# A three-layer graph attention kernel on one core: another PSUM bank for one pick a round, the first copy of picked tiles on VectorE, and node work after the picks

## The chip, the core and the metric

The kernel runs on one NeuronCore of a Trainium2 chip. Its engines each follow their own queue of instructions in order and meet only at semaphores: PE (TensorE, the matmuls; PEld is its weight loader), DVE (VectorE), ACT (ScalarE), POOL (GpSimd, here the issuer of gathers) and SP (SyncE, the issuer of most other transfers). Matmuls write into PSUM, which has eight banks of 2 KB a partition; VectorE and ScalarE read it from there. The metric is device time in microseconds (us) of one execution.

## The reference

The inputs are a graph of N = 6250 nodes with 64 features each, and 206250 edges sorted by destination, with 64 features each. Three layers of graph attention follow, then a residual and a layer norm.

```python
def _transformer_conv(x, src, dst, edge_attr, Wq, bq, Wk, bk, Wv, bv, We, Ws, bs):
    q = x @ Wq + bq
    k = x @ Wk + bk
    v = x @ Wv + bv
    e = edge_attr @ We
    kj = k[src] + e
    alpha = jnp.sum(q[dst] * kj, axis=-1) / jnp.sqrt(jnp.float32(D))
    amax = jax.ops.segment_max(alpha, dst, num_segments=N)
    p = jnp.exp(alpha - amax[dst])
    denom = jax.ops.segment_sum(p, dst, num_segments=N)
    w = p / denom[dst]
    msg = (v[src] + e) * w[:, None]
    agg = jax.ops.segment_sum(msg, dst, num_segments=N)
    return agg + x @ Ws + bs
...
for i in range(L):
    x = _transformer_conv(x, src, dst, edge_attr, Wq[i], bq[i], Wk[i], bk[i], Wv[i], bv[i], We[i], Ws[i], bs[i])
    x = jax.nn.relu(x)
    if i < L - 1:
        x = _layer_norm(x, ln_gamma[i], ln_beta[i])
return jax.nn.log_softmax(x, axis=1)
```

## The kernel before

**Units.** The edges are cut into chunks of 768 (six tiles of 128), and four chunks make a unit: 67 whole units and a rest. For each layer, `main_path` walks over the units in a loop whose body has four quarters, j = 0 to 3, one chunk each. All engines follow the order in which this loop is written; nothing reorders it later. Several units are in flight: while unit u is turned, unit u-1 is scored and weighted, unit u-2 is summed, and source rows are collected for unit u+1.

**What one unit needs.** `turn` (L1679, L1682) transposes the source rows of a chunk on PE and copies them out with ScalarE. `scores` (L1692) multiplies them with the queries, one half of the columns into bank `s` and the other into `s` (layer 0) or `m` (layers 1 and 2). `most` (L1706, L1719) takes the maximum of each half on VectorE, and after the second half ScalarE takes the exponential (L1720). `weights` (L1734, L1737) transposes the probabilities into bank `p` and copies them out; `sums` (L1746, L1753) makes the weighted sums. `store` writes a unit's partial results.

**Picks.** Source rows come in two ways. Most tiles are gathered by index with a transfer that POOL issues (L601), once ScalarE has copied its indices into a gate (L633). The others are picked: all node rows of a window lie on chip (`parts`), VectorE writes one-hot columns (L1335, by `aim`), and PE multiplies (L1387, eight matmuls a pick, by `Picker.batch`). A pick gives 2 tiles of 128 rows with 4 candidates each, side by side in one PSUM bank. `evacuate` keeps the right one: a copy of candidate 0 (L1356, on ScalarE), then three predicated copies of candidates 1 to 3 over it (L1359, on VectorE). Then the bank is free. After a pair's last pick ScalarE swaps half of its rows in three copies (L1346 to L1348).

**Layer 0** makes four picks a unit, one each quarter, in banks p, p, s, p (the string `ppsp`). It also has the sorter to run: the edge features are put in the order of the picks by one-hot matmuls (L1074 on VectorE, L1085 and L1094 on PE), a few steps each quarter by `move`, half of them ahead of the pick and half after it; `evacuate` is called after the second half. Bank `s` is shared with the scores there, and bank `p` with the probabilities.

**Layers 1 and 2** make six or seven picks a unit (2, 1, 2, 1 or 2, 2, 2, 1 in the quarters) in bank `x`, which has two buffers; each is evacuated right after it is issued.

**Node work.** Whenever all edges of a group of four node blocks are done, `finish` works through the group in small steps (L1499 to L1577), and, but for the last layer, `project` (L1432 to L1448) makes the next layer's queries. `step` runs one step of the node work that layer 0 has active; `close_up`, in quarter 0, runs that and one step of every group that is being finished. In layers 1 and 2 `step` finds nothing to do, so that only `close_up` matters there.

Of the kernel before, what the change touches and what calls it, by code (L numbers as in the profile page):

```python
# [32 lines left out]
LB = 4  # L33
# [396 lines left out]
def main_path(  # L430
# [53 lines left out]
    nc = tc.nc  # L484
# [815 lines left out]
    class Picker:  # L1300
# [49 lines left out]
        def evacuate(self):  # L1350

            if not self.late:
                return
            k, pair, t, px, which = self.late.pop()
            found = loaded[self.layer, k][:, 2 * pair : 2 * pair + 2, t, 0]
            nc.scalar.copy(found, px[:, :, 0])  # L1356
            first = t * LB + 2 * pair
            for b in range(1, KB):
                nc.vector.copy_predicated(  # L1359
                    found,  # L1360
                    which[:, first : first + 2, b].bitcast(I32).unsqueeze(2).to_broadcast([P, 2, D]),
                    px[:, :, b],
                )
            if t == self.plan[k][pair] - 1:
                self.swaps.append((k, pair, t + 1))
# [6 lines left out]
        def batch(self, k):  # L1372

            for pair, most in enumerate(self.plan.get(k, ())):
                for t in range(most):
                    if not self.layer:
                        self.swap()
                    self.aim()
                    at, hot = self.hots[k, t]
                    bank = "x" if self.layer else "ppsp"[self.quarter]  # L1380
                    px = ps(bank).rearrange("p (s b d) -> p s b d", s=2, b=KB)
                    for v in range(2):
                        w = t * WT + v
                        those, b0 = parts[w // HALF], w % HALF * WB
                        for h in range(NH):
                            for i in range(2):
                                nc.tensor.matmul(  # L1387
                                    px[:, v].rearrange("p b d -> p (b d)"),
                                    hot[:, h, (2 * pair + v) * P : (2 * pair + v + 1) * P],
                                    those[:, i, b0 + h * KB : b0 + (h + 1) * KB, :].rearrange("p b d -> p (b d)"),  # L1390
                                    start=(h == 0 and i == 0),
                                    stop=(h == NH - 1 and i == 1),
                                )
                    self.late.append((k, pair, t, px, self.which[k]))
                    if not any(t < more for more in self.plan[k][pair + 1 :]):
                        self.free.append(self.hots.pop((k, t))[0])
                    if self.layer:
                        due = len(self.swaps)
                        self.evacuate()
                        self.swap(len(self.swaps) - due)  # L1400
                    self.aim()
                    yield
            self.which.pop(k, None)
# [491 lines left out]
    for layer in range(L):  # L1895
# [3 lines left out]
        def free(u, j):  # L1899
            lead = 2 * LB if not layer else min(2 * LB, LB + u)  # L1900
            release(layer, u * LB + j + (0 if not layer else 1) + lead, nc.scalar.copy)

        picker = Picker(layer)
        for u in range(NU - 2):
# [11 lines left out]
            for j in range(LB):  # L1916
                picker.quarter = j
                if j == 2:
                    line.weights(u - 1, 0)
                this.turn(j)  # L1920
                if j == 0:
                    line.refill(u - 2)
                free(u, j)
                if j == 0:
                    if layer:
                        line.most(u - 1, 0)
                        line.products(u - 1, 1, "m")
                    close_up()
                else:
                    if j == 1:  # L1930
                        line.store()
                    step()
                a, b = -(-n * j // LB), -(-n * (j + 1) // LB)
                move(pace - pace // 2)
                if not layer and (not j or j == 1 and placed(0, u + 1)):
                    line.most(u - 1, j)
                for _ in range(b - a):
                    next(picking, None)
                move(pace // 2)
                if not layer:  # L1940
                    picker.evacuate()
                if j == 0:
                    if layer:
                        line.most(u - 1, 1)
                    else:
                        line.products(u - 1, 1)
                        if not placed(0, u + 1):
                            line.most(u - 1, 1)
                    ask(layer, u + 1)
                    chunks[layer, u + 1].across()  # L1950
                if j == 2:
                    line.weights(u - 1, 1)
                    chunks[layer, u + 1].shade()
                    decode(layer, u + 2)
# [21 lines left out]
        u = NU - 2  # L1976
# [117 lines left out]
```

## Time and profile before

| | us |
|---|---|
| median of three runs | 4764.53 |
| the three runs | 4761.85 to 4769.58 |
| profiled execution, its own time | 4768.13 |
| span of its instructions | 4766.3 |
| TensorE clock granted, mean | 0.873 |

Busy time over the span is 3718.2 us (78%) on PE, 3073.9 (64%) on DVE, 2548.1 (53%) on ACT and 2659.0 (56%) on POOL. The steady stretch of layer 0 runs from 180 to 2290 us, that of layer 1 from 2363 to 3480 and that of layer 2 from 3600 to 4680.

A group of the profile stands for all instructions of one line, engine and shape: after the count come busy us and mean ns of one, then the idle time of that engine just before them and what ended it. In a timeline, "[2.71 <-DVE feat L1359]" says that the engine had idled 2.71 us and that the instruction of L1359 on VectorE ended the wait. In the view of waits a line gives engine, what waited, whom it waited for, the total in us, how often, and the longest. A wait for several semaphores is put down to the one that came last. The granted clock is a share of TensorE's full clock.

### The profile page before, as it was taken

How to read it: one execution, taken by the hardware profiler on the slowest of the kernel's cores; microseconds unless marked ns; L12 is line 12 of the kernel's file. 1: busy time of each engine (PE TensorE's matmuls, PEld its weight loads, DVE VectorE, ACT ScalarE, POOL GpSimd, SP SyncE). 2: the span in 40 equal slices, each digit the busy share in tenths (PEclk: the TensorE clock that was granted, in tenths of full speed). 3: DMA queues.
4: the chain of work that ended last, by engine and by line, in shares of the span. 5: the costliest groups of instructions: out<-in, count | busy, mean ns of one | idle time of the engine just before them, and what ended most of it. 6: DMA issues, size and time to landing. Idle time of an engine off the chain costs nothing.

```text
span 4766.3 us, 108288 instructions
## 1 busy us (share of the span) xinstructions
PE 3718.2 (78%) x34711; PEld 2645.0 (55%) x34711; DVE 3073.9 (64%) x10790; ACT 2548.1 (53%) x6962; POOL 2659.0 (56%) x2642
## 2 busy tenths in 40 slices
PE   4888777887878878788588777878867887777786
PEld 2444444444444445445467666666646666666664
DVE  5576666666667666666456666666655666666665
ACT  1344444444444444445466666666646666666665
POOL 5464454555544544455376666666637666666663
PEclk9888888888888888889688899999879888888887
DMA  5655455455555545555566666666655666666663
GB/s 124 175 156 146 127 150 144 131 151 141 144 149 142 144 136 146 141 137 161 131 163 174 162 166 166 176 170 168 171 153 147 175 163 162 166 163 173 162 164 96
DMA packets 783502, 728.92 MB, mean 153 GB/s; under 512 B 485192, under 2 KB 610050, under 8 KB 782928
## 3 DMA queue, kind: packets, MB, share of 16 engines
q1 hardware_dynamic: 630436, 508.46, 40.4%
q0 software_dynamic: 84224, 86.41, 9.4%
q10 hardware_dynamic: 68268, 127.03, 7.4%
q8 instruction: 283, 4.64, 0.4%
q14 instruction: 291, 2.38, 0.2%
HBM read 562.78 MB, written 158.68 MB: 151 GB/s over the span
## 4 chain that ended last, share of the span: by engine, by line


## 5 line engine op out<-in xcount | busy, mean ns | idle before, releaser
L601 POOL DMA_INDIRECT feat<-x,gate x1460 | 1447.5, 991 | 776.5 <-ACT gate L633 363.7
L601 POOL DMA_INDIRECT feat<-in_x,gate x1100 | 1138.3, 1035 | 1115.4 <-ACT gate L633 823.2
L1387 PE MATMUL ps_x<-parts,hot 128*128 128x256 f32 x6864 | 1096.5, 316 | 307.3 <-DVE feat L1359 184.7
L1359 DVE COPY_PREDICATED feat<-which,ps_x 128x128 f32<-128x128 int32 x2574 | 766.0, 302 | 792.2 <-ACT feat L1356 704.7
L1387 PEld LDWEIGHTS ps_x<-parts,hot 128*128 128x128 f32 x6864 | 987.6, 218 | 410.5 <-issue 156.1
L1682 ACT COPY featT<-ps_a 64x384 f32<-64x384 f32 x1588 | 751.7, 473 | 320.6 <-PE ps_a L1679 309.3
L1734 PE MATMUL ps_p<-ident,prob 128*128 128x128 f32 x1197 | 246.3, 323 | 330.3 <-DVE feat L1359 202.1
L1679 PE MATMUL ps_a<-ident,feat 128*128 128x128 f32 x2380 | 453.7, 303 | 32.2 <-DMA feat<-x,src_b 31.3
L1335 DVE TENSOR_SCALAR hot<-keys,rank 128x512 fp32r<-128x512 f16 (+1 forms) x1172 | 471.1, 469 | 1.6 <-DMA keys<-keyS 1.6
L1074 DVE TENSOR_SCALAR hit<-ruler,pos 128x384 bf16<-128x384 f16 x1608 | 447.9, 320 | 14.2 <-PE ps_m L1094 14.2
L1679 PEld LDWEIGHTS ps_a<-ident,feat 128*128 128x128 f32 x2380 | 308.3, 155 | 210.7 <-issue 181.8
L1720 ACT ACTIVATE prob<-prob,part 128x768 f32<-128x768 f32 x204 | 190.2, 932 | 385.3 <-DVE part L1719 371.2
L1734 PEld LDWEIGHTS ps_p<-ident,prob 128*128 128x128 f32 x1197 | 156.6, 162 | 385.9 <-issue 230.1
L1359 DVE COPY_PREDICATED feat<-which,ps_p 128x128 f32<-128x128 int32 x552 | 165.6, 300 | 303.5 <-ACT feat L1356 289.7
L1085 PE MATMUL ps_x<-hit,raw 128*64 128x384 bf16 x1608 | 321.4, 395 | 0.7 <-DVE hit L1074 0.5
L1356 ACT COPY feat<-ps_x 128x128 f32<-128x128 f32 x858 | 221.9, 266 | 175.2 <-PE ps_x L1387 156.5
L1746 PE MATMUL ps_g<-feat,probT 128*32 128x128 f32 x9672 | 312.8, 276 | 0.8 <-ACT probT L1737 0.8
L1085 PE MATMUL ps_x<-hit,rest 128*64 128x384 bf16 x1608 | 303.9, 374 | 0.0
L1085 PE MATMUL ps_x<-hit,end 128*64 128x384 bf16 x1608 | 301.4, 371 | 0.0
L1692 PE MATMUL ps_s<-featT,q 128*32 128x384 f32 x2134 | 249.7, 511 | 44.5 <-DVE most L1706 26.4
L1746 PEld LDWEIGHTS ps_g<-feat,probT 128*32 128x32 f32 x9672 | 262.6, 110 | 25.1 <-ACT probT L1737 2.5
L1737 ACT COPY probT<-ps_p 128x384 f32<-128x384 f32 x399 | 192.7, 483 | 129.7 <-PE ps_p L1734 126.5
(266 smaller groups left out, 5230.0 us busy)
## 6 DMA issues: line engine op xcount, KB each, us to landing
featT<-eaS SPq DMA_DIRECT2D x792, 192.0 KB
feat<-eaP SPq DMA_DIRECT2D x134, 768.0 KB
raw<-in_ea SPq DMA_DIRECT2D x536, 96.0 KB
eaS<-eT ACTq DMA_DIRECT2D x134, 384.0 KB
eaP<-feat ACTq DMA_DIRECT2D x128, 384.0 KB
shade<-maskS SPq DMA_DIRECT2D x198, 192.0 KB
keys<-keyS SPq DMA_DIRECT2D x66, 448.0 KB
keys<-keyS SPq DMA_DIRECT2D x66, 384.0 KB
```

The costliest lines, as they stand in the source:

```text
L601: nc.gpsimd.indirect_dma_start(out=feat[:, c, t, 0], out_offset=None, in_=xts[layer][:, :], in_offset=bass.IndirectOffsetOnAxis(ap=index[: ...
L1074: nc.vector.tensor_scalar(hit, ruler, self.pos[:, at : at + 1], None, ALU.is_equal)
L1085: nc.tensor.matmul(self.px[j * D : (j + 1) * D, :HE], self.parts[2 * h + i].thirds[part][:, j, t * D : (t + 1) * D], self.hits[h, 2 * i + ...
L1335: nc.vector.tensor_scalar(hot[:, h], keys[self.layer, k][:, first : first + n], rank[:, h : h + 1], None, ALU.is_equal)
L1356: nc.scalar.copy(found, px[:, :, 0])
L1359: nc.vector.copy_predicated(found, which[:, first : first + 2, b].bitcast(I32).unsqueeze(2).to_broadcast([P, 2, D]), px[:, :, b],)
L1387: nc.tensor.matmul(px[:, v].rearrange("p b d -> p (b d)"), hot[:, h, (2 * pair + v) * P : (2 * pair + v + 1) * P], those[:, i, b0 + h * KB ...
L1679: nc.tensor.transpose(pt[:, t * P : (t + 1) * P], rows[:, 2 * t * D : 2 * (t + 1) * D], ident)
L1682: nc.scalar.copy(featT[:, :, h, :], pt[h * D : (h + 1) * D, : n * P].rearrange("d (i e) -> d i e", e=P))
L1692: nc.tensor.matmul(p_s[rows, :w], self.q[:, rows], self.featT[j][:, cols], start=True, stop=True)
L1734: nc.tensor.transpose(p_t[:, t, :n], self.prob[:n, at : at + P], ident[:n, :n])
L1746: nc.tensor.matmul(p_g[rows, :].rearrange("n (h d) -> n h d", h=2), self.probT[:, t, rows], batch[:, j, t], start=(t == 0), stop=(t == sel ...
```

## The change

Three edits, all in `main_path`. First, `evacuate` makes the copy of candidate 0 on VectorE. Second, in layer 0 the second pick of a unit goes to bank `s` in place of `p`; the second half's `most` moves ahead of `step` and of the sorter's steps in quarter 1, since that pick needs the bank which `most` reads. Third, in layers 1 and 2 the picks of a quarter come straight after its turn, and `close_up` or `step` after the picks; in quarter 0 the second half's `most` now stands behind the first pick, and no longer behind all picks of the quarter.

```diff
@@ evacuate
-            nc.scalar.copy(found, px[:, :, 0])
+            nc.vector.tensor_copy(found, px[:, :, 0])
@@ batch
-                    bank = "x" if self.layer else "ppsp"[self.quarter]
+                    bank = "x" if self.layer else "pssp"[self.quarter]
@@ the loop over quarters
                 free(u, j)
+                if j == 0 and layer:
+                    line.most(u - 1, 0)
+                    line.products(u - 1, 1, "m")
+                if j == 1:
+                    line.store()
+                    if not layer and placed(0, u + 1):
+                        line.most(u - 1, 1)
+                a, b = -(-n * j // LB), -(-n * (j + 1) // LB)
+                if layer:
+                    for i in range(max(b - a, 1)):
+                        next(picking, None)
+                        if not i and not j:
+                            line.most(u - 1, 1)
                 if j == 0:
-                    if layer:
-                        line.most(u - 1, 0)
-                        line.products(u - 1, 1, "m")
                     close_up()
                 else:
-                    if j == 1:
-                        line.store()
                     step()
-                a, b = -(-n * j // LB), -(-n * (j + 1) // LB)
-                move(pace - pace // 2)
-                if not layer and (not j or j == 1 and placed(0, u + 1)):
-                    line.most(u - 1, j)
-                for _ in range(b - a):
-                    next(picking, None)
-                move(pace // 2)
                 if not layer:
+                    move(pace - pace // 2)
+                    if j == 0:
+                        line.most(u - 1, 0)
+                    for _ in range(b - a):
+                        next(picking, None)
+                    move(pace // 2)
                     picker.evacuate()
                 if j == 0:
-                    if layer:
-                        line.most(u - 1, 1)
-                    else:
+                    if not layer:
                         line.products(u - 1, 1)
                         if not placed(0, u + 1):
                             line.most(u - 1, 1)
```

On PE in layer 0 this is the second pick of one unit, between two steps of the sorter (`hot` are the one-hot columns, `parts` the node rows, `ps_p` and `ps_s` the banks):

```order
 L1094 LDWEIGHTS stamp_259
 L1094 MATMUL ps_m<-hit,stamp_259 32x384
-L1387 MATMUL ps_p<-parts,hot_18028 128x256 x8
+L1387 MATMUL ps_s<-parts,hot_18028 128x256 x8
 L1128 MATMUL ps_a<-ident,eT 128x128 x3
 L1085 LDWEIGHTS raw
```

The pick keeps its place in PE's order and changes its bank. On VectorE in layer 0, at the end of quarter 0 of a unit, the first pick leaves its bank and the second maximum follows:

```order
 L989 TENSOR_SCALAR spare<-spare 128x96
 L991 TENSOR_SCALAR spare<-spare 128x96
-L1359 COPY_PREDICATED feat<-which,ps_p 128x2x64 x3
+L1356 COPY feat<-ps_p 128x2x64
+L1359 COPY_PREDICATED feat<-which,ps_p 128x2x64 x3
+L1706 ISA prob,most<-ps_s,shade,most 128x384
+L1706 ISA most 128x1
+L1719 TENSOR_SCALAR part<-most 128x1
 L1074 TENSOR_SCALAR hit<-ruler,pos 128x384 x2
 L1042 TENSOR_TENSOR rest<-raw 128x384
```

The copy of L1356 has come to this engine, and the maximum of the second half (L1706, L1719) stands right behind the first pick; before, it stood eleven rows further on, behind the sorter's work of quarter 1. On VectorE in layer 1, quarter 0 of a unit with node work (L1519 and below are `finish`):

```order
 L1706 ISA prob,most<-ps_s,shade 128x384
 L1706 ISA most 128x1
+L1356 COPY feat<-ps_x 128x2x64
+L1359 COPY_PREDICATED feat<-which,ps_x 128x2x64 x3
+L1706 ISA prob,most<-ps_m,shade,most 128x384
+L1706 ISA most 128x1
+L1719 TENSOR_SCALAR part<-most 128x1
+L1356 COPY feat<-ps_x 128x2x64
+L1359 COPY_PREDICATED feat<-which,ps_x 128x2x64 x3
 L1519 TENSOR_TENSOR el<-mm,both 128x8
 L1522 TENSOR_TENSOR has<-el 128x4
```

Both picks of the quarter and the second maximum now stand ahead of the seven instructions of node work of this unit; before, they stood behind them, and the second maximum behind both picks.

## The prediction

> **What bounds the kernel now.** I read the busy time by stage first. The rows below are layer 0 and the steady parts of layers 1 and 2; the columns are the stretch, its length, and busy microseconds (with instruction counts) of PE, the weight loader, VectorE (DVE), ScalarE (ACT) and GpSimd (POOL), then the granted TensorE clock and DMA.
> ```profile
> core 0: us, PE busy (x) PEld busy (x) DVE busy (x) ACT busy (x) POOL busy (x), PEclk, DMA share, GB/s
> 180.00:2290.00 2110.00, 1703.95 (x15463) 1010.97 (x15466) 1412.28 (x5044) 1007.57 (x2675) 1075.94 (x1042) 0.86 0.53 145
> 2363.00:3480.00 1117.00, 899.04 (x8860) 745.76 (x8864) 715.79 (x2436) 686.77 (x1972) 731.79 (x739) 0.91 0.64 167
> 3600.00:4680.00 1080.00, 862.21 (x8545) 725.11 (x8546) 699.19 (x2400) 691.02 (x1942) 697.19 (x703) 0.89 0.64 166
> ```
> PE is busiest in every stage, at about 80%, so what matters is who ends PE's idle time: 406 us in layer 0, 218 us in each later layer. The view of waits, for PE alone, says it. Layer 0 (300 to 2280 us):
> ```profile
> PE ps_p L1734 <- DVE feat L1359: 200.3, 59, 5.1
> ```
> Layer 1 (2370 to 3480 us):
> ```profile
> PE ps_x L1387 <- DVE feat L1359: 100.9, 81, 2.8
> PE ps_p L1734 <- ACT prob L1720: 57.3, 53, 1.9
> PE ps_x L1387 <- ACT feat L1348: 31.7, 24, 2.5
> ```
> Layer 2 (3600 to 4690 us):
> ```profile
> PE ps_x L1387 <- DVE feat L1359: 83.7, 66, 3.5
> PE ps_x L1387 <- ACT feat L1348: 81.6, 39, 4.1
> PE ps_p L1734 <- ACT prob L1720: 52.8, 43, 1.9
> ```
> Columns are total, times, longest. Layer 0 has one wait that is half of all PE idle time: the transposes of the probabilities (L1734) want bank p, which a pick still holds. The later layers have 298 us at picks that wait for a bank of x (a pick's tile leaves it with L1359; the swaps of L1348 only end beside that), and 110 us for the exponential of L1720.
>
> **Layer 0, the bank.** One round around 1020 us, in order of time (start, length, engine, line):
> ```profile
> 1019.56 1.21 PE L1387 MATMUL ps_p<-parts,hot 128*128 128x256 f32 x8
> 1019.60 0.61 DVE L1706 CUSTOM_DVE_ANT_0 prob<-ps_s,shade,most 128x384 f32<-128x384 f32 x1
> ...
> 1020.44 0.94 ACT L1720 ACTIVATE prob<-prob,part 128x768 f32<-128x768 f32 x1 [1.18 <-DVE part L1719]
> ...
> 1023.26 0.28 ACT L1356 COPY feat<-ps_p 128x128 f32<-128x128 f32 x1
> ...
> 1023.58 0.97 DVE L1359 COPY_PREDICATED feat<-which,ps_p 128x128 f32<-128x128 int32 x3 [2.71 <-ACT feat L1356]
> ...
> 1024.69 0.52 PE L1734 MATMUL ps_p<-ident,prob 128*128 128x128 f32 x3 [2.71 <-DVE feat L1359]
> ...
> 1026.56 1.21 PE L1387 MATMUL ps_s<-parts,hot 128*128 128x256 f32 x8
> ```
> The second pick ends at 1020.8, yet its tile leaves bank p only at 1024.55: VectorE idles 2.71 us for a copy that stands in ScalarE's queue. PE then stands 2.71 us too, although the probabilities were ready at 1021.4. With that pick in bank s, L1734 needs of p only what the first quarter's pick left long before. Bank s takes the second pick once the second maximum (L1706) has read it, and that is now queued ahead of the quarter's other VectorE work. The third pick, also in s, must wait for the second's copies. It started at 1026.56, two sorting steps after L1734, so with PE 2.7 us earlier it would want s at 1023.9, 0.7 us before the copies ended; but those no longer queue on ScalarE, so they end some 2 us earlier. Of 200.3 us I take 170; bounds 0 (the wait moves to the third pick or to L1720) and 200.
>
> **Layer 0, the clock.** After such a stall PE is given a lower clock. Seven stalls in a row, the 3.4 us after each (clock: third number from the end):
> ```profile
> 1024.60:1028.00 3.40, 3.31 (x30) 2.49 (x32) 2.24 (x8) 2.31 (x7) 0.94 (x1) 1.00 1.11 215
> 1057.60:1061.00 3.40, 3.40 (x14) 1.68 (x14) 1.70 (x6) 2.22 (x7) 0.52 (x1) 0.50 1.06 236
> 1100.20:1103.60 3.40, 3.32 (x18) 2.04 (x18) 2.33 (x8) 2.14 (x7) 0.44 (x1) 0.50 0.50 166
> 1132.60:1136.00 3.40, 3.34 (x19) 2.12 (x19) 2.22 (x8) 2.17 (x7) 0.46 (x1) 0.56 1.12 247
> 1162.40:1165.80 3.40, 3.36 (x19) 1.90 (x20) 2.20 (x8) 2.41 (x7) 0.94 (x1) 0.58 1.03 246
> 1194.10:1197.50 3.40, 3.30 (x14) 1.70 (x14) 1.79 (x6) 2.13 (x7) 0.43 (x1) 0.50 0.89 270
> 1234.60:1238.00 3.40, 3.38 (x18) 2.03 (x18) 2.17 (x8) 2.21 (x7) 0.51 (x1) 0.50 0.55 170
> ```
> Mean 0.59, so 1.4 us of each stretch is lost; 59 times 1.4 is 83. The shorter idle gaps that stay may trip it too: I take 70, bounds 0 and 120. [...]
>
> **The first copy on VectorE.** These are groups by line: count, then busy and mean ns, then the idle time before them.
> ```profile
> L1359 DVE COPY_PREDICATED feat<-which,ps_x 128x128 f32<-128x128 int32 x2574 | 766.0, 302 | 792.2 <-ACT feat L1356 704.7 <-ACT gate L633 12.6 <-DMA feat<-x,gate 10.1
> L1359 DVE COPY_PREDICATED feat<-which,ps_p 128x128 f32<-128x128 int32 x552 | 165.6, 300 | 303.5 <-ACT feat L1356 289.7 <-ACT feat L1348 1.0
> L1359 DVE COPY_PREDICATED feat<-which,ps_s 128x128 f32<-128x128 int32 x180 | 54.4, 302 | 245.9 <-ACT feat L1356 241.7
> L1356 ACT COPY feat<-ps_x 128x128 f32<-128x128 f32 x858 | 221.9, 266 | 175.2 <-PE ps_x L1387 156.5 <-issue 3.0
> L1005 DVE COPY spare<-ps_a 128x96 f32<-128x96 f32 x16 | 3.9, 244 | 0.0
> L776 DVE COPY qs<-ps_a 64x128 f32<-64x128 f32 x3 | 0.8, 276 | 2.8 <-DMA qq<-qs 2.8
> ```
> VectorE takes 244 copies in layer 0 (552 + 180 over 3) and 858 later. Its nearest rows for a copy out of PSUM are 244 ns (96 columns) and 276 ns (128 columns, half the partitions): I take 276, so 304 us in all, 67 of them in layer 0, and ScalarE loses 266 ns each. In layer 0 that lies under the 531 us (289.7 + 241.7) in which VectorE stood waiting for ScalarE: nothing on the path; without that cover, 67. [...]
>
> **Layers 1 and 2.** One unit of layer 1 with no node work in it:
> ```profile
> 2706.07 3.17 DVE L1335 TENSOR_SCALAR hot<-keys,rank 128x512 fp32r<-128x512 f16 x8
> ...
> 2707.70 2.17 PE L1387 MATMUL ps_x<-parts,hot 128*128 128x256 f32 x16
> ...
> 2709.16 0.54 DVE L1706 CUSTOM_DVE_ANT_0 prob<-ps_s,shade 128x384 f32<-128x384 f32 x1
> ...
> 2709.64 2.02 DVE L1359 COPY_PREDICATED feat<-which,ps_x 128x128 f32<-128x128 int32 x6
> ...
> 2710.75 2.24 PE L1387 MATMUL ps_x<-parts,hot 128*128 128x256 f32 x16 [0.55 <-ACT feat L1356]
> ...
> 2712.40 0.94 ACT L1720 ACTIVATE prob<-prob,part 128x768 f32<-128x768 f32 x1 [1.75 <-DVE part L1719]
> ...
> 2714.69 1.84 DVE L1359 COPY_PREDICATED feat<-which,ps_x 128x128 f32<-128x128 int32 x6 [2.33 <-ACT feat L1356]
> ...
> 2715.81 3.59 PE L1387 MATMUL ps_x<-parts,hot 128*128 128x256 f32 x16 [1.45 <-DVE feat L1359]
> ...
> 2719.88 1.19 PE L1387 MATMUL ps_x<-parts,hot 128*128 128x256 f32 x8
> ```
> I put the new order on it. VectorE is late here because of the eight one-hot tiles: the maximum still ends at 2709.7. Emptying the first pick now takes 0.3 + 1.0 = 1.3 us, to 2711.0, where it took 1.0; the second maximum (0.8 us with its reductions) then lets L1720 start at 2711.9 instead of 2712.4; the second pick leaves at 2713.2 instead of 2711.7. So picks 3 and 4 end at 2714.3, later than the 2713.0 of before: 1.3 us lost. Now the gain: before, VectorE idled 2.33 us until 2714.69, because the copy of pick 3 stood behind L1720 and the copies of the turn on ScalarE. Without that, pick 3 leaves at 2714.5, and picks 5 and 6, behind transposes (0.4) and a turn (0.4), start at 2715.15 instead of 2715.81 with no wait. If PE then has its full clock they take 2.2 us as at 2707.70, not 3.59. The unit gains 0.65 to 2.0 us. Where node work is due, its VectorE work now stands ahead of pick 3's copy, not pick 1's, and ScalarE's node work behind L1720: it hides under picks 1 and 2, but the stall returns at pick 5, which waits for that copy. The transfers and gathers keep their order on SP and POOL, so no queue there is passed. I take 0.7 us a unit, 128 units: 90 us. Bounds: a loss of 1.3 a unit, 166 us, if nothing comes back; a gain of all 408 us of waits. VectorE's sum does not forbid a gain: 715.79 + 422 copies of 276 ns (1266 rows of L1359 in layer 1, over 3) is 832 of 1117 us, but it becomes the nearest engine behind PE, which is why I stay far under 408.
>
> **Sum.** 4768.13 (the profiled run, 1.8 over its span of 4766.3) less 170, 70, 0 and 90 is 4438. That run lies 3.6 above the median of the three, so against the median I say 4434.
>
> **Rivals.** (1) Layers 1 and 2 give nothing, because the copies on VectorE eat what the earlier exponential brings; layer 0 pays: 4765 - 240 = 4525. For it speaks the unit above, up to pick 4. (2) Most waits go: layer 0 gives its bounds, 200 + 120, and the later layers half of their 408 us: 4765 - 524 = 4241. For it, VectorE's 704.7 us of waiting for ScalarE at the picks of x; against it, VectorE's 832 us. (3) The wait of layer 0 only moves, to the third pick in bank s: that gives back 200 of the 240; 4765 - 40 - 90 = 4635. Against it, the 531 us that VectorE gets back just there. (4) Slower: VectorE, late behind the one-hot tiles and the sorting, becomes the bound, and every copy lies on the path at 0.31 us (0.276 and the gap to the next): 1102 of them are 340 us, the layers' waits stay, and layer 0's stall comes back as waiting for VectorE: 4765 + 340 = 5105. It decides once the copies on the path cost more than the bank brings, from 240 / 0.31 = 770 of 1102 on. Against it, VectorE is busy 67% in layer 0 and 64% in layer 1. That the change does not do what it says is out: the order above shows bank s at the second pick and the copy on VectorE.
>
> **Chances.** The forecast 0.50, its own range 4340 to 4520; (1) 0.20; (2) 0.16; (3) 0.08; (4) 0.04; no net effect 0.02. The range for all, 4240 to 4640, leaves out (4), the far end of (2) and some of (3). A measurement tells 0.2%, 9.5 us. Faster: 0.50 + 0.20 + 0.16 + 0.08 = 0.94, less 0.02 for (3) with layers 1 and 2 losing besides, half of it to each side: 0.92; same 0.02 + 0.01 = 0.03; slower 0.04 + 0.01 = 0.05.
>
> **What would show it.** In the waits of layer 0, L1734 for L1359 gone, and L1387 in bank s for L1359 near zero; the clock of layer 0 above 0.86; the stretch to the first layer 1 pick some 240 us shorter. In the groups, VectorE's copy at L1356 near 276 ns and the idle time before it ended by PE, not ScalarE. In layers 1 and 2, the wait of L1734 for L1720 mostly gone, that of L1387 for VectorE still there, perhaps half. I am wrong if L1734 waits as long for L1720, if PE begins to wait for the hits of L1074, or if VectorE passes 85% in layers 1 and 2 with PE's waits no smaller.

## The result and the profile after

| | before, us | after, us |
|---|---|---|
| median | 4764.86 (4 runs) | 4360.84 (4 runs) |
| lowest to highest | 4761.85 to 4769.58 | 4353.09 to 4365.19 |
| profiled execution | 4768.13 | 4357.57 |
| TensorE clock granted, mean | 0.873 | 0.926 |

The ratio is 0.9149, with a 95% interval of 0.9133 to 0.9166. The change brings 404 us; the forecast had 331 (4765 to 4434), and its range held the time.

Where the 404 us are: I take the first VectorE instruction of each unit (`which`, L1324) and count from a layer's first unit to its last; the first two units of layers 1 and 2 and the last of layer 0, which lie at the layers' boundaries, are left out.

| first to last unit, us | layer 0 | layer 1 | layer 2 |
|---|---|---|---|
| before | 2070.2 | 1076.3 | 1088.3 |
| after | 1720.0 | 1045.8 | 1048.4 |
| difference | -350.2 | -30.5 | -39.9 |

The differences add up to 420.6 us, and the two profiled executions lie 410.6 apart, so what is outside these stretches took 10 us longer. Layer 0 gave more than its 240, and the later layers a little less than their 90. The busy time of the changed kernel by stage, in the columns that the prediction used, for the steady parts of layers 0, 1 and 2:

```profile
180.00:1935.00 1755.00, 1553.10 (x15422) 935.04 (x15419) 1488.31 (x5282) 951.43 (x2421) 1114.44 (x1037) 0.94 0.65 174
2008.00:3090.00 1082.00, 887.41 (x8798) 702.73 (x8799) 824.12 (x2847) 588.72 (x1537) 730.76 (x736) 0.94 0.68 172
3210.00:4265.00 1055.00, 854.80 (x8596) 675.30 (x8594) 811.75 (x2832) 606.49 (x1549) 705.86 (x710) 0.95 0.67 171
```

In layer 0 PE does the same work (15422 records, 15463 before) in 355 us less (2110 - 1755). Its idle time falls from 406 to 202 us, and its busy time from 1703.95 to 1553.10. The second part goes with the clock: busy time by granted clock is 1703.95 x 0.86 = 1465 before and 1553.10 x 0.94 = 1460 after. VectorE is at 85%, 76% and 77% of the three stretches. The waits of PE in layer 0 after, largest first, begin with

```profile
PE ps_a L1128 <- DVE kbs L1184: 20.8, 12, 3.4
PE ps_a L923 <- DVE kinds L916: 19.7, 10, 3.2
```

so that the 200 us of L1734 for L1359 are gone; the third pick in bank s waits 0.3 us in all. The groups of the changed kernel's page, to be read like those of before:

```profile
L1387 PE MATMUL ps_x<-parts,hot 128*128 128x256 f32 x6864 | 1033.1, 299 | 173.5 <-DVE feat L1359 157.3
L1359 DVE COPY_PREDICATED feat<-which,ps_x 128x128 f32<-128x128 int32 x2574 | 779.0, 303 | 88.7
L1356 DVE COPY feat<-ps_x 128x128 f32<-128x128 f32 x858 | 246.2, 287 | 301.4 <-PE ps_x L1387 295.6
```

The first copy is now VectorE's, 287 ns each, and VectorE idles ahead of it for PE; the predicated copies no longer wait (792.2 us of idle time before them, now 88.7). In layers 1 and 2 the waits of PE have changed places. Layer 1 (2010 to 3050 us) after:

```profile
PE ps_x L1387 <- DVE feat L1359: 59.8, 74, 2.0
PE ps_s L1692 <- issue: 44.2, 16, 4.6
PE ps_s L1692 <- DMA featT<-eaS: 25.0, 13, 3.8
...
PE ps_p L1734 <- ACT prob L1720: 10.4, 21, 0.5
```

Layer 2 (3190 to 4230 us) after:

```profile
PE ps_x L1387 <- DVE feat L1359: 86.3, 99, 2.6
PE ps_s L1692 <- issue: 48.9, 20, 4.0
PE ps_s L1692 <- DMA featT<-eaS: 29.2, 14, 3.9
PE ps_p L1734 <- ACT prob L1720: 12.4, 25, 0.5
```

The transposes' wait for the exponential has fallen from 110 us to 23, and the picks' from 298 to 146. A wait of the scores (L1692) has grown from 12 us (5.8 and 3.9 in layer 1, 2.1 and 0.5 in layer 2) to 147 in both layers together: for the load of their edge features (`featT`), or, where the row says "issue", for nothing that the profile names (one such wait, of 3.43 us, ends at 2505.37, 1.4 us after SyncE issued such a load at 2503.96, so that the load is likely what it waited for). The lengths of the units have spread as well. The tenth and ninetieth percentile of a unit's length were 15.4 and 18.7 us in layer 1 and are 13.7 and 21.2; in layer 2 15.4 and 19.0, now 13.1 and 20.7. The quick units became quicker by about 2 us, and the long ones slower by about as much.

One long unit of layer 2, SyncE's queue of the changed kernel (start, length, line):

```profile
3427.58 0.33 SPq L570 DMA_DIRECT2D feat<-eaP  x1
3437.66 0.39 SPq L1575 DMA_DIRECT2D out<-y  x1
3438.57 2.81 SPq L1633 DMA_DIRECT2D q<-qq  x4
3441.50 1.79 SPq L1659 DMA_DIRECT2D featT<-eaS  x2
3443.54 3.76 SPq L1757 DMA_DIRECT2D part<-part  x4
```

and of VectorE and PE in the same unit:

```profile
3431.19 3.19 PE L1387 MATMUL ps_x<-parts,hot 128*128 128x256 f32 x16
...
3436.44 0.17 DVE L1472 RECIPROCAL dev<-dev 128x4 f32<-128x4 f32 x1
3436.64 0.99 DVE L1474 TENSOR_SCALAR y<-y,mv,dev 128x64 f32<-128x64 f32 x4
...
3446.21 0.83 PE L1692 MATMUL ps_s<-featT,q 128*32 128x384 f32 x2 [1.88 <-DMA featT<-eaS]
```

SyncE stands 9.7 us, from 3427.9 to 3437.66, ahead of the store of finished output rows (L1575), because VectorE makes those rows (L1474) behind both picks of the quarter. Behind that store stand the next unit's queries (L1633) and edge features (L1659), and PE waits for edge features until 3446.21. All such stores together, in SyncE's waits of layer 2 after:

```profile
SPq L1575 <- DVE top L1501: 47.6, 5, 10.1
SPq L1575 <- DVE y L1474: 30.1, 4, 8.4
```

77.7 us in nine stores. The same two rows of the kernel before (layer 2, 3600 to 4680 us) have 41.5:

```profile
SPq L1575 <- DVE top L1501: 23.6, 5, 5.0
SPq L1575 <- DVE y L1474: 17.9, 4, 4.7
```

Whether this is a cost of the third edit, the experiments had to show.

### The profile page after: what moved, and what is told of

It reads as the page before. It is cut to its first block, busy times and chain, and to the rows that moved or that the text cites. A ratio compares the mean times of both kernels' runs of the same rounds, so it can differ in the third digit from the quotient of the medians.

```text
span 4355.8 us, 108102 instructions
## 1 busy us (share of the span) xinstructions
PE 3555.1 (82%) x34711; PEld 2476.2 (57%) x34711; DVE 3376.9 (78%) x11892; ACT 2305.6 (53%) x5860; POOL 2706.5 (62%) x2642
## 4 chain that ended last, share of the span: by engine, by line
## 5 line engine op out<-in xcount | busy, mean ns | idle before, releaser
L601 POOL DMA_INDIRECT feat<-x,gate x1460 | 1451.2, 994 | 706.4 <-issue 315.6
L601 POOL DMA_INDIRECT feat<-in_x,gate x1100 | 1181.8, 1074 | 724.0 <-ACT gate L633 421.0
L1387 PE MATMUL ps_x<-parts,hot 128*128 128x256 f32 x6864 | 1033.1, 299 | 173.5 <-DVE feat L1359 157.3
L1387 PEld LDWEIGHTS ps_x<-parts,hot 128*128 128x128 f32 x6864 | 905.8, 199 | 326.7 <-issue 231.2
L1359 DVE COPY_PREDICATED feat<-which,ps_x 128x128 f32<-128x128 int32 x2574 | 779.0, 303 | 88.7
L1356 DVE COPY feat<-ps_x 128x128 f32<-128x128 f32 x858 | 246.2, 287 | 301.4 <-PE ps_x L1387 295.6
L1692 PE MATMUL ps_s<-featT,q 128*32 128x384 f32 x2134 | 306.3, 505 | 191.2 <-issue 104.6
L1679 PEld LDWEIGHTS ps_a<-ident,feat 128*128 128x128 f32 x2380 | 285.1, 147 | 251.6 <-issue 190.2
L1720 ACT ACTIVATE prob<-prob,part 128x768 f32<-128x768 f32 x204 | 190.3, 933 | 251.1 <-DVE part L1719 155.8
L1746 PE MATMUL ps_g<-feat,probT 128*32 128x128 f32 x9672 | 315.3, 276 | 2.0 <-ACT probT L1737 2.0
L1085 PE MATMUL ps_x<-hit,rest 128*64 128x384 bf16 x1608 | 281.1, 346 | 0.0
L1746 PEld LDWEIGHTS ps_g<-feat,probT 128*32 128x32 f32 x9672 | 262.9, 111 | 27.8 <-ACT probT L1737 5.7
L1734 PE MATMUL ps_p<-ident,prob 128*128 128x128 f32 x1197 | 212.3, 288 | 37.1 <-ACT prob L1720 33.8
L1692 PEld LDWEIGHTS ps_s<-featT,q 128*32 128x32 f32 x2134 | 71.2, 111 | 267.2 <-issue 194.2
L1706 DVE CUSTOM_DVE_ANT_0 prob<-ps_s,shade 128x384 f32<-128x384 f32 x204 | 112.9, 553 | 129.6 <-PE ps_s L1692 120.3
```

Source lines behind the costliest of these rows:

```text
L601: nc.gpsimd.indirect_dma_start(out=feat[:, c, t, 0], out_offset=None, in_=xts[layer][:, :], in_offset=bass.IndirectOffsetOnAxis(ap=index[: ...
L1085: nc.tensor.matmul(self.px[j * D : (j + 1) * D, :HE], self.parts[2 * h + i].thirds[part][:, j, t * D : (t + 1) * D], self.hits[h, 2 * i + ...
L1356: nc.vector.tensor_copy(found, px[:, :, 0])
L1359: nc.vector.copy_predicated(found, which[:, first : first + 2, b].bitcast(I32).unsqueeze(2).to_broadcast([P, 2, D]), px[:, :, b],)
L1387: nc.tensor.matmul(px[:, v].rearrange("p b d -> p (b d)"), hot[:, h, (2 * pair + v) * P : (2 * pair + v + 1) * P], those[:, i, b0 + h * KB ...
L1679: nc.tensor.transpose(pt[:, t * P : (t + 1) * P], rows[:, 2 * t * D : 2 * (t + 1) * D], ident)
```

## The experiments

Three edits make the change: the bank with its earlier maximum (layer 0), the copy on VectorE (all layers), the node work behind the picks (layers 1 and 2). The runs took them apart, and then tried cures for the new wait. The bank and its earlier maximum were not parted; in the round of the prediction the probabilities were ready 3 us before bank p was free, so the maximum is not what L1734 waited for there. The ratios are to the kernel before on the same chip, with 95% intervals.

### Four parts on another chip

The first four runs fell on a chip on which the kernel before took 5967.65 us (median of 19 runs, 5941 to 6009), a quarter more than elsewhere. The edits, taken from the diff above:

```diff
# e1_bank: the kernel before, and only
-                    bank = "x" if self.layer else "ppsp"[self.quarter]
+                    bank = "x" if self.layer else "pssp"[self.quarter]
                     if j == 1:
                         line.store()
+                        if not layer and placed(0, u + 1):
+                            line.most(u - 1, 1)
                     step()
...
-                if not layer and (not j or j == 1 and placed(0, u + 1)):
+                if not layer and not j:
                     line.most(u - 1, j)
# e2_copy: the kernel before, and only
-            nc.scalar.copy(found, px[:, :, 0])
+            nc.vector.tensor_copy(found, px[:, :, 0])
# e3_node: the kernel before with the third edit only (layers 1 and 2)
# e4_bank_copy: the edits of e1_bank and e2_copy together
```

> Only the bank of layer 0's second pick changes, with the second maximum moved ahead of quarter 1; the first copy stays on ScalarE. Layer 0 (from its first unit to its last) took 2070 us before and takes 1720 in the changed kernel. Theory A (the bank is the cause by itself): the wait of L1734 for L1359 goes, and layer 0 falls by 240 us or more, to 1830 or less; total near 4520. Rival B (the bank only helps together with the copy): the third pick, also in bank s, waits for the second's copies because they still queue on ScalarE; layer 0 falls by under 120 us, L1387 shows a wait on L1359 of 100 us or more; total 4645 or more. Layers 1 and 2 must stay within 10 us of before.

> Only the first copy goes to VectorE, in all layers; banks and order as before. Theory A: the layer 0 stall is mostly the copy's time in ScalarE's queue, so it shrinks by about half (59 stalls of 3.4 us to about 1.7) and layer 0 falls by 100 to 200 us; layers 1 and 2 fall by 40 to 100 each from the 2.3 us that VectorE idled each unit; total 4400 to 4580. Rival B (VectorE becomes the bound): layers 1 and 2 stay or rise, layer 0 falls by under 60; total 4700 or more.

> Only the order in layers 1 and 2 (picks before node work, second maximum behind the first pick); copy on ScalarE and bank p as before. Theory A (the order alone brings little: the maximum comes earlier and takes up to 110 us of waits for L1720, but node work then stands ahead of the queue's next loads): total between 4720 and 4790. Rival B (the order is what makes layers 1 and 2 faster): 70 us or more off layers 1 and 2, total 4695 or less. Layer 0 must stay within 10 us of before.

> The changed kernel without its third edit: bank and copy, node work ahead of the picks in layers 1 and 2 as before. Theory A (in the changed kernel the node work behind the picks delays SP's loads for the next unit, which gives back what the quick units win): layers 1 and 2 are as fast or faster than in the changed kernel (1046 and 1048 us by the first and last unit), total 4300 to 4365. Rival B (the third edit earns the gain of layers 1 and 2): they are slower, 1065 or more each, total 4390 or more. Layer 0 as in the changed kernel, 1720.

| | us, median | ratio |
|---|---|---|
| e1_bank | 5862.37 (4 runs) | 0.9822 (0.9764 to 0.9880) |
| e2_copy | 5943.50 (10 runs) | 0.9954 (0.9925 to 0.9983) |
| e3_node | 5891.20 (4 runs) | 0.9875 (0.9813 to 0.9937) |
| e4_bank_copy | 5899.10 (10 runs) | 0.9887 (0.9855 to 0.9920) |

None of these medians gains the 2% that count as a clear change, and none of the expected times holds here. Something else costs time on this chip. PE's timeline of e1_bank through the short matmuls of the weighted sums (L1746) of one unit:

```profile
4519.95 1.10 PE L1746 MATMUL ps_g<-feat,probT 128*32 128x128 f32 x22
4521.43 0.27 PE L1746 MATMUL ps_g<-feat,probT 128*32 128x128 f32 x1 [0.38 <-issue]
4522.16 0.41 PE L1746 MATMUL ps_g<-feat,probT 128*32 128x128 f32 x3 [0.46 <-issue]
4522.86 0.27 PE L1746 MATMUL ps_g<-feat,probT 128*32 128x128 f32 x1 [0.29 <-issue]
...
4528.05 0.41 PE L1746 MATMUL ps_g<-feat,probT 128*32 128x128 f32 x1 [0.82 <-issue]
```

48 such matmuls in the kernel before on its own chip:

```profile
4028.98 1.52 PE L1746 MATMUL ps_g<-feat,probT 128*32 128x128 f32 x48
```

8.5 us instead of 1.5, in bursts some 0.75 us apart that wait for nothing the profile shows ("issue"). How much this is in all can be read by comparing e1_bank with e11_bank below, which is the same kernel on a chip like the first. The groups of these matmuls, e1_bank first:

```profile
L1746 PE MATMUL ps_g<-feat,probT 128*32 128x128 f32 x9672 | 722.8, 319 | 512.6 <-issue 498.0
L1746 PE MATMUL ps_g<-feat,probT 128*32 128x128 f32 x9672 | 312.5, 276 | 0.9 <-ACT probT L1737 0.9
```

Busy time and idle time of this one group are 922 us longer, of the 1376 us by which the two spans differ (5872.4 and 4496.0). What makes these matmuls come late on that chip was not found. These runs therefore say nothing of the sizes on the other chips, and the parts were run again, but for the third edit alone: it brings 1.2% here, and by itself it was not run elsewhere.

### The parts on chips like the first

Beside all runs that follow the kernel before took 4760 to 4765 us (medians), as at first. The bank alone and the copy alone are the kernels of above; the bank with the copy is the change without its third edit.

> The kernel before with the second edit alone: in layer 0 the second pick goes to bank s and the second maximum goes ahead of quarter 1's step and sorting; ScalarE still makes the first copies. The prediction's account puts layer 0's whole gain here, 240 (170 for the bank, 70 for the clock): 4500 to 4550. Rival, now the likelier as layer 0 gained 350: the second pick still waits for ScalarE's copy, so a part of the stall moves to the third pick in the same bank, and the bank alone brings 80 to 200: 4560 to 4680, with L1387 in bank s waiting for VectorE's L1359 more than 40 us in layer 0.

> The kernel before with the first edit alone: VectorE makes the first copy of the picks in all layers. The prediction gave it nothing in layer 0 and put it into the 90 of the later layers together with the third edit: then 4670 to 4760. Rival: it takes ScalarE's queue out of the way from pick to free bank, and so shortens layer 0's wait for bank p (200 us) by a third to two thirds and gives the later layers all they gained: 4530 to 4640, layer 0 shorter by 70 to 180 and layers 1 and 2 together by 100 to 140 (first to last unit: before 2070, 1076 and 1088).

> The changed kernel without its third edit: layers 1 and 2 are ordered as in the kernel before, with the first copy on VectorE; layer 0 is that of the changed kernel (its second maximum ahead of the step of node work of quarter 1 too). It gives the third edit by itself, as the distance to 4361. My theory: the quiet units of layers 1 and 2 win by the copy on VectorE alone about half of what they won, and the third edit's gain in quiet units is nearly given back in the units with node work: 4340 to 4400 where the kernel before takes 4765, L1734's wait for L1720 in layers 1 and 2 together still above 50 us. Rival, the prediction's account that the third edit brings the gain of these layers: 4410 to 4450. If the kernel before takes 5950 us, the first four runs' kernels stand again: 5880 to 5920.

> The changed kernel itself, beside the others on one chip: 4350 to 4370 where the kernel before takes 4762, so that the 4309, 4320, 4305 and 4314 of its four variants stand as gains of 40 to 55. If it gives 4310 to 4330 here, those gains were the chip's.

| | us, median of 4 | ratio | layer 0 | layer 1 | layer 2 |
|---|---|---|---|---|---|
| e11_bank | 4487.11 | 0.9413 (0.9398 to 0.9429) | 1795.2 | 1079.3 | 1083.6 |
| e12_copy | 4390.76 | 0.9218 (0.9192 to 0.9244) | 1792.6 | 1048.0 | 1009.1 |
| e8_bank_copy | 4314.02 | 0.9060 (0.9015 to 0.9106) | 1721.9 | 1037.8 | 1005.2 |
| e9_again (the whole change) | 4352.63 | 0.9139 (0.9110 to 0.9167) | 1711.9 | 1049.0 | 1046.2 |

The layers are from first to last unit, as above. **Layer 0:** the bank alone takes off 275 us and the copy alone 278, but both 348: they cure the same stall in two ways. Both single times lie below every range that was expected for them (4500 to 4550 and 4560 to 4680 for the bank, 4670 to 4760 and 4530 to 4640 for the copy): what either edit does to layer 0 without the other had been put too low. With the bank alone L1734 no longer waits for L1359. With the copy alone that wait stays, shorter; the copy alone has, in layer 0 (300 to 2005 us),

```profile
PE ps_p L1734 <- DVE feat L1359: 61.0, 53, 3.3
```

53 waits of 1.2 us in place of 59 of 3.4. Both leave PE's clock higher than the 0.86 of before, at 0.93 and 0.92. Layer 0 of the bank alone, then of the copy alone:

```profile
180.00:2015.00 1835.00, 1581.11 (x15449) 946.68 (x15448) 1412.56 (x5043) 1000.87 (x2674) 1102.91 (x1042) 0.93 0.62 167
```

```profile
180.00:2012.00 1832.00, 1593.04 (x15437) 949.10 (x15437) 1485.82 (x5282) 955.34 (x2427) 1085.73 (x1039) 0.92 0.62 167
```

Against 1703.95 busy of 2110, the bank alone brings 123 us of busy time and 152 of idle time, the copy alone 111 and 167.

The rival on the third pick also fell. With the bank alone, L1387 in bank s waits for L1359 only this long in layer 0 (300 to 2005 us), although ScalarE still makes the first copy:

```profile
PE ps_s L1387 <- DVE feat L1359: 21.6, 41, 1.0
```

**Layers 1 and 2:** the bank alone does nothing there (-2 us together), the copy alone takes off 107.5, the copy beside the bank 121.6 (the bank has no part in these layers, so that the two differ by what runs differ). The whole change takes off 70.4 in the first run and 69.4 in the second. **The third edit costs time**: 4314 without it, 4353 and 4361 with it, about 1%, and the intervals (to 0.9106, from 0.9110 and 0.9133) just do not meet. The 4314 of the copy beside the bank is below both ranges that were expected (4340 to 4400 and 4410 to 4450), as both gave the third edit a share in the gain. The layers say where it loses. Layer 2 takes 1005.2 and 1009.1 us without it and 1048.4 and 1046.2 with it. In layer 1 no loss is shown: 1037.8 and 1048.0 without it, 1045.8 and 1049.0 with it, and 1038.6 in e10_later below, whose layer 1 is that of the changed kernel.

Its trade shows in the waits of PE in e8_bank_copy, which lacks it. Layer 1 (2010 to 3050 us):

```profile
PE ps_p L1734 <- ACT prob L1720: 62.6, 55, 1.7
PE ps_x L1387 <- DVE feat L1359: 60.2, 56, 2.5
PE ps_s L1692 <- issue: 19.3, 12, 4.1
PE ps_s L1692 <- DMA featT<-eaS: 17.9, 6, 3.5
```

Layer 2 (3190 to 4230 us):

```profile
PE ps_x L1387 <- DVE feat L1359: 65.0, 59, 2.7
PE ps_p L1734 <- ACT prob L1720: 63.7, 57, 1.7
PE ps_s L1692 <- issue: 24.2, 20, 4.0
PE ps_s L1692 <- DMA featT<-eaS: 10.9, 6, 2.6
```

The copy without the third edit already brings the picks' wait from 298 us to 125 (127 with the copy alone, 146 with the whole change), and the scores' wait from 12 to 72. The tenth percentile of a unit's length is 13.6 and 13.5 us with the copy alone, so the quick units are the copy's work too. What the third edit adds differs by layer. In layer 1 it takes 52 us off the wait for the exponential and puts 32 on the scores'. In layer 2 it takes off 51, and puts 43 on the scores' wait and 21 on the picks'. PE's idle time in layer 2, from first to last unit, is 198.6 us with it and 168.8 without, its busy time 849.8 and 836.4; these two make up the 43 us by which the layer is longer.

### Cures for the new wait

Three kernels change only layers 1 and 2 of the changed kernel, and a fourth one line of its last layer.

```diff
# e5_ask: the next unit's requests ahead of the node work
+                if j == 0 and layer:
+                    ask(layer, u + 1)
+                    chunks[layer, u + 1].across()
                 if j == 0:
                     close_up()
# e6_ahead: the node work ahead of the picks again
                 if layer:
+                    if j == 0:
+                        close_up()
+                    else:
+                        step()
                     for i in range(max(b - a, 1)):
                         next(picking, None)
# e7_both: requests, then node work, then picks
# e10_later: the changed kernel, the output's store one unit later
         yield from norm(y, n, None, not at_end and g + 2 * GS > NB)
         full = min(n, N // P - g)
+        if not at_end:
+            yield
         if full:
             nc.sync.dma_start(out[g * P : (g + full) * P, :]...
```

(In e5 and e7 the requests at their old place stay for layer 0 alone.)

> The changed kernel, but in layers 1 and 2 the requests for the next unit (its masks, keys and collected features, SyncE's transfers) are made ahead of the node work of quarter 0, and no longer behind it. In the changed kernel TensorE waits for SyncE's transfers at the scores (L1692) some 150 us in layers 1 and 2 together, a wait that was not there before, and units with node work take 20 to 28 us where quiet ones take 13.7. My theory: SyncE's queue has been passed by the edit, because the requests now stand behind the node work's own stores and loads, and this costs most of these 150 us. Then the wait of L1692 falls under 60 us and the time, where the kernel before takes 4765, is 4230 to 4310 (changed kernel: 4361). Rival: SyncE is simply full in these units (its serial chain of small loads and stores is the same in any order), so the wait moves to another load: 4340 to 4380, and L1692's wait or another for a load keeps 100 us or more. If the kernel before takes 5950 us, as in the first four runs, TensorE's sums (L1746) are starved there and the two may differ by under 30 us.

> The changed kernel, but in layers 1 and 2 the node work of quarter 0 stands again ahead of the picks, as in the kernel before; the second maximum stays behind the first pick. My theory: what layers 1 and 2 gained in quiet units comes from the earlier second maximum and the copy on VectorE, not from the place of the node work, and the place of the node work costs in the units that have it what SyncE's requests lose behind it. In this kernel the requests stand behind the node work too, but the picks do as well, so the wait of L1692 for SyncE's transfers stays, and the stall of the first pick behind the node work comes back: 4370 to 4430 where the kernel before takes 4765. Rival: the place of the node work is worth nothing at all and only the maximum's place counts: 4350 to 4370. A second rival, in which the place of the node work behind the picks is itself what hurts: 4290 to 4340.

> The changed kernel with both of the last two edits: in layers 1 and 2 the next unit's requests first, then the node work, then the picks of quarter 0, with the second maximum behind the first pick. On its own, the earlier request gave 4309 and the earlier node work 4320, against 4361 for the changed kernel (kernel before 4760). Theory that both cure the same ill (what stands behind the node work in SyncE's and the other queues comes too late): no more than either alone, 4295 to 4325. Rival, that they cure two things, the late transfers of the scores (L1692) and the late node work that the sums of the next units wait for: the gains add up, 4255 to 4285. If either gain was only scatter between runs: 4330 to 4370.

> The changed kernel with one line more: in the last layer the store of a finished group's rows (L1575, on SyncE) is issued one step, that is one unit, later than the VectorE work that makes the rows; the last group's store stays. In the changed kernel SyncE waits 78 us in layer 2 at this store for VectorE (top L1501 and y L1474, up to 10.1 us at once), because that work now stands behind the picks, and the next unit's loads queue behind the store; in the variant without the third edit it is 32 us. My theory, that the third edit loses its time by blocking SyncE there: this wait falls under 15 us, layer 2 shortens from 1048 to about 1010 (between first and last unit) and the time to 4300 to 4330. Rival: the store is only where a lateness of the whole node work shows, and the next unit's loads wait as long for something else: 4345 to 4370, with SyncE waiting at another line of the node work.

| | us, median | ratio | layer 1 | layer 2 | SyncE at L1575 in layer 2 |
|---|---|---|---|---|---|
| whole change (e9_again) | 4352.63 (4 runs) | 0.9139 (0.9110 to 0.9167) | 1049.0 | 1046.2 | 76.1 |
| e5_ask | 4309.44 (2 runs) | 0.9050 (0.8999 to 0.9101) | 1034.9 | 1010.2 | 38.5 |
| e6_ahead | 4320.15 (2 runs) | 0.9073 (0.9044 to 0.9101) | 1059.9 | 1006.2 | 32.0 |
| e7_both | 4305.06 (4 runs) | 0.9016 (0.8969 to 0.9062) | 1037.8 | 1008.4 | 4.4 |
| e10_later | 4291.14 (4 runs) | 0.9004 (0.8962 to 0.9046) | 1038.6 | 1003.7 | 2.3 |

**e5_ask** came out at the edge of its theory's range (4230 to 4310; its two runs are 4299.76 and 4319.13), and against its mechanism: the scores' wait was to fall under 60 us and is 129 in the windows where the changed kernel has 147. What fell is SyncE's wait at the store. Of the gain 38 us lie in layer 2 (1048.4 to 1010.2) and 11 in layer 1, the latter no more than layer 1 differs between e9_again and e10_later, which have it the same. **e6_ahead** fell on the second rival (4290 to 4340): the place of the node work behind the picks is itself what hurts. It wins in layer 2 alone. **e7_both** gives no more than either alone, as its theory had it (4295 to 4325): one ill, cured twice. **e10_later**, below the 4300 to 4330 of its theory, is the test by itself. It leaves the node work behind the picks, leaves the requests behind the node work, and only moves the store out of the unit in which its rows are made. SyncE's waits at the store in layer 2, of e9_again and then of e10_later (where the line has moved by the two that were added):

```profile
SPq L1575 <- DVE top L1501: 46.2, 5, 10.0
SPq L1575 <- DVE y L1474: 29.9, 4, 8.0
```

```profile
SPq L1577 <- DVE hot L1335: 2.3, 4, 0.8
```

Layer 2 falls from 1046.2 to 1003.7. Layer 1, which is the same in both kernels (its own store of rows already stands one step later), is 10 us shorter and layer 0, also the same, 13 us longer; by that much a layer can differ from run to run. The rival, that SyncE would wait as long at another line of the node work, fell: no such line comes up in its waits of layer 2 (27 us more are waited at the stores of partial results, 77.2 for 49.8, behind a load). So in layer 2 the loss is the store that blocks SyncE's queue, and this is shown by the one line that was moved. The way from there to PE is seen only in part: the scores' wait in layer 2 falls from 67 us to 48, which is 20 of the 42. The runs of this kernel scatter by 37 us (4278.08 to 4315.31), as those of e7_both and e8_bank_copy do, and it cannot be told from e7_both, e5_ask or e8_bank_copy. It is faster than both kernels of this study, 61 us under the changed one on the same chip.

## Why the prediction was right, and where it was wrong

**The bank.** Right in mechanism, and near in size: the idle time of layer 0 fell by 204 us (406 to 202) with all edits and by 152 with the bank alone, where the term was 170 with 200 as its upper bound. The stall did not move to the third pick (rival 3): 0.3 us there after.

**The clock.** This is the term that was mis-sized: 70, bounds 0 and 120. The busy time of layer 0 fell by 151 us at a granted clock of 0.94 instead of 0.86. I had counted the 3.4 us after each of the 59 long stalls (83 us) and no more, and had taken the shorter gaps for a reason to go lower; that the low clock ends after 3.4 us was my assumption, and no run shows it. After two of the seven stalls that the prediction shows, the clock of the kernel before stayed at 0.50 for much longer than that, 9.7 us:

```profile
1057.60:1067.30 9.70, 9.70 (x39) 4.81 (x40) 3.47 (x10) 2.88 (x8) 3.78 (x4) 0.50 0.50 115
1194.10:1203.80 9.70, 9.60 (x39) 4.83 (x40) 3.57 (x10) 2.88 (x8) 3.77 (x4) 0.50 0.40 110
```

The stage's own rows gave the estimate that I should have used as the bound: 1703.95 us at a clock of 0.86 leave 1703.95 x 0.14 = 239 us to win, if busy time times clock stays the same, as it nearly did (1465 and 1460). Of the 110 us that layer 0 brought beyond its 240, most are the 81 between 70 and 151. That the stalls lower the clock is read from the two going together in the runs of layer 0, and not shown by itself: of the seven stretches after stalls one has a clock of 1.00, and the others 0.50 to 0.58. The stalls of 1.2 us that the copy alone leaves go with a clock of 0.92.

**The first copy.** Its cost was right: 287 ns against the 276 taken, and it does not show in layer 0, which is 73 us shorter with the copy beside the bank than with the bank alone. That it brings nothing to layer 0 by itself was wrong: alone it gives 278 us there. The text had the reason at hand ("those no longer queue on ScalarE, so they end some 2 us earlier") and used it only for the third pick. As the bank cures the same stall, the pair gives 348 and not 553, so the sum of layer 0 did not suffer by it; a forecast for the bank alone or the copy alone would have. The copy is 21 ns dearer on VectorE than on ScalarE, 287 ns against 266, paid 858 times in the later layers. These still win.

**Layers 1 and 2.** The size was near, 70 against 90, and that is in part luck: one term held two edits, of which one won more than the term and the other lost. The unit that I worked through had its loss, 1.3 us, where the second maximum and the longer emptying hold back picks 3 and 4, and its gain where pick 3's copy no longer stands in ScalarE's queue. That gain was right, and it belongs to the copy: the copy alone takes 107 us off, 122 beside the bank, and the quick units with it alone are 1.8 and 1.9 us shorter, within the 0.65 to 2.0 that were forecast. Rival (1) had this the other way round, with the earlier exponential as the gain and the copies as the price. What the sum lacked is a price for the third edit, which gives 51 us of the 122 back, 43 of them in layer 2.

**The step that failed** in these layers is the sentence "The transfers and gathers keep their order on SP and POOL, so no queue there is passed". The order was kept: in layer 1 the traces of the two kernels have the same 1002 transfers of SyncE one after another. But a store in that order waits for VectorE, and the edit moved what it waits for behind two picks. SyncE stood 77.7 us at these stores in layer 2 in place of 41.5, up to 10.1 us at once in place of 5.0, and what is behind them in its queue came later with them. I asked of each moved step which transfers it issues, and not which transfers already in the queue wait for it. And I said of the node work only that "the stall returns at pick 5"; of its own stores nothing.

**The rivals.** (1) fell, since layers 1 and 2 gave 70. (2), 4241 with most waits gone, is nearer to what the best variant reached (4291) than to the change. (4) fell: VectorE reaches 85% in layer 0, and PE's idle time there halved. Of the signs named, L1734 for L1720 mostly gone and the picks' wait at about half both came (110 to 23, and 298 to 146, the second by the copy); the first unit of layer 1 came 350 us earlier, not 240.

## What to carry to other kernels

When work is moved later on one engine, look through the other queues for each instruction that waits for that work and ask what stands behind it: here SyncE's queue, which stood 77.7 us at nine stores of layer 2 in place of 41.5, passed the delay on to loads that have nothing to do with it, and one line that issues the store a step later won 61 us in the medians, 42 of them in the layer that has the store. Two edits that cure the same stall must be costed as one stall, not as two terms (here 348 us for the pair, not 553). What a lower clock costs is better estimated by the stage's busy time times what its mean clock lacks (here 239 us, of which 151 came) than by the stretches after the longest stalls (83 us).

## What the hardware showed unexpectedly

One of the chips that ran these kernels took 5968 us for a program that took 4760 to 4765 on the others, steadily (19 runs within 1.2%). Its VectorE copies are no slower (302 ns for L1359 there, 302 before), nor are POOL's gathers (975 ns of L601 against 991); what differs most is that PE's shortest matmuls arrive in bursts, 8.5 us for 48 of them in the place shown, and 922 us in all between two runs of one kernel. On that chip the bank and the copy together bring 1.1% and on another 9.4%, so what an edit is worth can depend on the chip, and the time of the kernel before beside each run is what tells.
